# Four graph attention layers on one core: two groups of nodes are projected for layer 1 while layer 0 still gathers

## The chip, the cores and the metric

The kernel runs on one core of a Trainium2 chip. The metric is the device time of one execution in microseconds (us), from the first to the last instruction. Five engines work side by side, each through its own queue in order: TensorE (PE, matmuls; its weight loads are listed as PEld), VectorE (DVE), ScalarE (ACT), GpSimd (POOL) and SyncE (SP, which only starts transfers here). An engine that waits for a semaphore holds up all that stands behind in its queue.

## The reference

Four residual blocks over a graph of 3327 nodes with 256 features and a sparse symmetric adjacency with self loops (about 1% of the entries are set). Each is `x = layernorm(x + attention(x, adj))`:

```python
# layer 0: score_ij = sum_c a_c * leaky_relu(g_src[i,c] + g_tgt[j,c]);  softmax over j with adj_ij != 0;  weights @ g_tgt
x = layernorm(x + L0(x, adj))
# layer 1: Wh = x @ W.T; e_ij = leaky_relu(Wh_i.a1 + Wh_j.a2, 0.2); masked softmax; attention @ Wh
x = layernorm(x + L1(x, adj))
# layer 2: H = x @ W_fc + b; scores_ij = H_i.w1 + H_j.w2 (no leaky_relu); masked softmax; alpha @ H
x = layernorm(x + L2(x, adj))
# layer 3: two GAT layers with 4 heads of 64 features, each elu(masked softmax(leaky_relu(f1_i + f2_j)) @ h)
x = layernorm(x + L3(x, adj))
```

## The kernel before

Nodes are cut into 26 tiles of 128 (the last has 127). All arithmetic is float32 but for layer 2's sums, which take each feature as three bfloat16 parts.

**Layer 0 (`sparse0`)** doesn't form the dense scores, as they depend on all 256 channels of a pair. It finds each node's neighbours (`neighbours`, DVE), sorts the nodes of a group by their number of neighbours, and gathers the neighbours' rows from a table in DRAM: one indirect DMA on GpSimd for 128 rows (L527), 8 to a buffer `g` (L525), 11 buffers in turn. The nodes form three groups (`SETS`) of 5, 9 and 12 tiles. For each buffer DVE makes scores (L546, L552); at the end of a tile ACT takes the exponent and scales the gathered rows (L633), and PE sums them (L636, an identity as one operand). The result plus the input goes back to its place by an indirect DMA to `sums_d` (`put_back`, L671); once a group is whole it is read into `h` (`take`), and normalized (`finish_sums`, `finish_root`, `finish`). A hand-written table of due steps (`at_step`) sets the order: a step is one gather buffer. In this part the program's order is kept on PE, DVE, ACT and POOL.

**Layers 1 to 3 (`layers`)** are dense. With `leaky_relu` of a sum, exp(leaky(s_i + t_j)) splits: the weight of a pair is, up to a factor of the row that the softmax removes, `max(rate_i, q_j) * adj_ij`, times a factor that is put into the features of j. So DVE makes `e = max(rate, q) * at` in one instruction for a tile j and a block of rows (`weigh`, L1075), and PE adds `e.T @ feat` into PSUM (`one_head`, L1159; `many_heads`, L1198 and L1206 for the sums of the weights). The rows i form four blocks of 7, 7, 6 and 6 tiles; for each block the loop runs over all 26 tiles j. In layer 1 the adjacency comes as int32 (`at_i`, 448 KB a tile of 7), ACT turns it into bfloat16 and stores it (`at_d`, L1092), and the later layers read that.

A layer needs, of each tile of nodes, its features: `turn` transposes `h` on PE, ACT copies it (`ht`, L1107), `project` multiplies by the weights on PE (L1011) and ACT takes the exponents and scales (L1018, L1019, L1023). And it needs `rate`, a number for each node and head, laid out along the free axis and the same on every partition. `rates_of` makes it: a matmul with the source weights as the stationary operand gives rows of 1 or 4 partitions (L1048), ACT takes the exponent (L1053), SyncE writes the rows to DRAM (L1057) and reads them back as a broadcast to all partitions (L1064).

These preparations for the next layer are generators in a list `pending`; the main loops take one step of it after each tile j from the fifth on (`work_off`, `LATER`), or as many as are needed until a feature or a rate is there (`work_until`). For layer 1 there is no loop before it: the preparation of its first block stands alone between layer 0 and layer 1, and the other blocks' go between the first block's steps. In layers 1 and 2 PE alone is kept in the program's order, in layer 3 PE, DVE and ACT. In `finish_hidden`, which ends a block of the first of layer 3's two parts, the steps of a unit of two tiles are staged: `spread`, three steps later `scale` (which also sets off two ACT exponents), then `elu` on DVE (L1299) and `project`:

```python
yield from staged(units, [(0, spread), (3, scale), (4, elu), (5, project)])
```

After layer 3 a flag decides whether a dense fallback runs; with these inputs it doesn't.

Of the kernel before, what the change touches and what calls it, by code (L numbers as in the profile page):

```python
# [19 lines left out]
P = 128  # L20
# [26 lines left out]
def gat_stack(  # L47
# [55 lines left out]

    def copy_rows(engine, dst, src):

        rows = dst.shape[0]
        whole = rows // 16 * 16
        for lo, hi in ((0, whole), (whole, rows)):
            if lo < hi:
                engine.dma_start(dst[lo:hi], src[lo:hi])  # L110
# [7 lines left out]
    def load_row(work, src, name):  # L118

        size = src.shape[0]  # L120
        t = work.tile([P, size], F32, tag="row_" + name, name=name, bufs=1)
        nc.sync.dma_start(
            t, bass.AP(tensor=src.tensor, offset=src.offset, ap=[[0, P], [1, size]])
        )
        return t
# [124 lines left out]
    def sparse0(lost):  # L250
        GROUP, TURNS, LEAD = 8, 11, 4
        starts = [sum(SETS[:s]) for s in range(len(SETS))]
        with ExitStack() as s0:
# [21 lines left out]
            for c in range(kc):  # L275
                t = io0.tile([P, dim], F32, tag="hs", name="dots0")
                nc.vector.tensor_mul(t, w_tgt[:, c, :dim], a_row)
                nc.vector.tensor_reduce(w_tgt[:, c, dim : dim + 1], t, axis=AX.X, op=ALU.add)
# [228 lines left out]
            ]  # L507
            held = {}
# [4 lines left out]
            def gather(q):  # L513
                (s, t), k0, k1 = parts[q]
                if k0 == 0:
                    entry = held[s, t] = {"g": []}
                    lst = listed[s][:, t, :]
                    own = io0.tile([P, OWN], F32, tag="own", name="own_of", bufs=4)
                    nc.gpsimd.indirect_dma_start(
                        out=own[:, :], out_offset=None, in_=own_d[s][:, :],  # L520
                        in_offset=bass.IndirectOffsetOnAxis(ap=lst[:, KMAX : KMAX + 1], axis=0),
                    )
                    entry["lst"], entry["own"] = lst, own
                entry = held[s, t]
                g = gath.tile([P, GROUP, ROW], F32, tag=f"g{q % TURNS}", name="g")  # L525
                for k in range(k0, k1):
                    nc.gpsimd.indirect_dma_start(  # L527
                        out=g[:, k - k0, :], out_offset=None, in_=table_d[:, :],
                        in_offset=bass.IndirectOffsetOnAxis(
                            ap=entry["lst"][:, k : k + 1], axis=0  # L530
                        ),
                    )
                    if k % 2 and between:
                        between.pop(0)()
                entry["g"].append(g)
# [76 lines left out]
            def combine(s, t):  # L612
# [30 lines left out]
                for g, k0, m in groups[-1:] + groups[:-1]:  # L643
                    for k in range(m):
                        scale(g[:, k, :dim], k0 + k)
                    if m % 2:
                        singles.append(g[:, m - 1, :dim])
                    for k in reversed(range(0, m - 1, 2)):
                        left -= 1
                        add_up(acc, g[:, k : k + 2, :dim], left == kt // 2 - 1, left == 0)  # L650
                        while singles:
                            add_up(acc[:, len(singles) - 1, :], singles.pop(), False, False)
# [34 lines left out]
            def finish_sums(s):  # L687

# [4 lines left out]
                for k, it in enumerate(block):  # L693
# [3 lines left out]
                    nc.vector.bn_aggr(mv[:pn, k, :], stats[:pn])  # L697
                rstd = small.tile([P, max(SETS)], F32, tag="rstd0", name="rstd0", bufs=2)
# [10 lines left out]
            def finish(s):  # L709
                mv, rstd = moments.pop(s)  # L710
                for k in range(SETS[s]):
# [5 lines left out]
                    )  # L717

# [25 lines left out]
            for q, key in ends.items():  # L744
                at_step(q + 4, add_input, *key)
                at_step(q + 6, between.append, lambda key=key: put_back(*key))
                if key[1] == SETS[key[0]] - 1:
                    at_step(q + 10, take, key[0])
                    at_step(q + 13, finish_sums, key[0])
                    at_step(q + 16, finish_root, key[0])  # L750
                    at_step(q + 18, finish, key[0])
            for it in range(SETS[0]):
# [36 lines left out]
            assert not between  # L789

# [182 lines left out]
    def layers(rs):  # L973
# [16 lines left out]
        class Layer:  # L990


            def __init__(self, name, slot, nh, leaky, load, bias=None):
                self.slot, self.nh, self.leaky, self.bias = slot, nh, leaky, bias
                self.weight = work.tile([P, kc, dim + nh], F32, tag="weight", name=name + "w")
                row_src, row_dst = load(self.weight)
                dots(work, self.weight[:, :, dim : dim + nh], self.weight, row_dst, nh)
                if leaky:
                    self.w_src = work.tile([P, kc, nh], F32, tag="w_src", name="w_src")
                    dots(work, self.w_src, self.weight, row_src, nh)  # L1000
                    self.rate_d = dram.tile([heads, n], F32, name=f"rate_{slot}{nh}_d")
# [3 lines left out]
            def project(self, j, ht, banks):  # L1005
# [4 lines left out]
                for k in range(kc):  # L1010
                    nc.tensor.matmul(  # L1011
                        pacc[:pn, : dim + nh], ht[:, k, :pn], self.weight[:, k, :],
# [3 lines left out]
                if self.leaky:  # L1016
# [5 lines left out]
                    for lo in range(0, dim, width):  # L1022
# [3 lines left out]
                        )  # L1026
                else:
# [12 lines left out]
            def rates_of(self, b, ht, banks):  # L1040


                c0, c1 = cols_of(blocks[b])
                for lo in range(0, c1 - c0, BANK):
                    hi = min(lo + BANK, c1 - c0)
                    pr = misc(banks)
                    for k in range(kc):
                        nc.tensor.matmul(  # L1048
                            pr[: self.nh, : hi - lo], self.w_src[:, k, :], ht[:, k, lo:hi],
                            start=(k == 0), stop=(k == kc - 1),  # L1050
                        )
                    row = work.tile([heads, BANK], F32, tag="spread", name="rate_row", bufs=4)
                    nc.scalar.activation(  # L1053
                        row[: self.nh, : hi - lo], pr[: self.nh, : hi - lo], AF.Exp,
                        scale=1.0 - SLOPE,
                    )
                    nc.sync.dma_start(  # L1057
                        self.rate_d[: self.nh, c0 + lo : c0 + hi], row[: self.nh, : hi - lo]
                    )
# [3 lines left out]
                rows = self.rate_d[: self.nh, c0:c1]  # L1063
                nc.sync.dma_start(  # L1064
                    rate[:, : self.nh, : c1 - c0], rows[None].to_broadcast([P, self.nh, c1 - c0])
# [30 lines left out]
        def turn(b, banks):  # L1096

            ht = turn_p.tile([P, kc, wide], F32, tag="ht", name="ht")
            for it in blocks[b]:
                pn = rows_of(it)  # L1100
                at0 = (it - blocks[b][0]) * P
                tp = misc(banks)
                for k in range(kc):
                    nc.tensor.transpose(  # L1104
                        tp[:, k * P : k * P + pn], h[it][:pn, k * P : (k + 1) * P], ident[:pn, :pn]
                    )
                nc.scalar.copy(  # L1107
                    ht[:, :, at0 : at0 + pn],
                    tp[:, : kc * P].rearrange("p (k i) -> p k i", k=kc)[:, :, :pn],
                )  # L1110
                yield ht, it

        def prepare(nxt, b, banks, normed=True):
# [3 lines left out]
            for ht, it in turn(b, banks):  # L1117
                at0 = (it - blocks[b][0]) * P
                yield
                nxt.project(it, ht[:, :, at0 : at0 + P], banks)  # L1120
                yield
            if nxt.leaky:
                nxt.rates_of(b, ht, banks)
# [19 lines left out]
        def one_head(layer, nxt, banks_next):  # L1143

            for b, block in enumerate(blocks):
                work_until(lambda: not layer.leaky or layer.rate[b] is not None)
                accs = [bank(s) for s in range(len(block))]
                for j in range(nt):
# [17 lines left out]
                    if j >= LATER:  # L1166
                        work_off()
                work_until(lambda: not pending)
                for s, it in enumerate(block):
# [6 lines left out]
                    )  # L1176
                pending.append(prepare(nxt, b, banks_next, normed=False))
# [82 lines left out]
        def finish_hidden(b, o, sums):  # L1260
# [47 lines left out]
            yield from staged(units, [(0, spread), (3, scale), (4, elu), (5, project)])  # L1308
            l3b.rates_of(b, o, (6, 7))
# [61 lines left out]
        def load_plain(w, row_src, row_dst):  # L1371
            def load(t):
                nc.sync.dma_start(t[:, :, :dim], w.rearrange("(c p) f -> p c f", p=P))
                return load_row(work, row_src, "src"), load_row(work, row_dst, "dst")
# [3 lines left out]
        def load_heads(w, a):  # L1378
            def load(t):
# [6 lines left out]
                for s, name in enumerate(("src", "dst")):  # L1386
                    r = work.tile([P, dim], F32, tag="row_" + name, name=name, bufs=1)
# [12 lines left out]
        l1 = Layer("l1", "f", 1, True, load_plain(l1_w_t, l1_a[:dim], l1_a[dim:]))  # L1400
        for b in range(len(blocks)):
            pending.append(prepare(l1, b, (7,)))
        work_until(lambda: l1.rate[0] is not None and not pending)
        l2 = Layer(
            "l2", "g", 1, False, load_plain(l2_w, l2_att[:dim], l2_att[dim:]), load_row(work, l2_b, "bias")
        )
        rs.enter_context(tc.manual_schedule(engines={mybir.EngineType.PE}))
        one_head(l1, l2, (7,))
        l3a = Layer("l3a", "f", heads, True, load_heads(l3_w1, l3_a1))
        one_head(l2, l3a, (7,))  # L1410
# [7 lines left out]
        l3b = Layer("l3b", "g", heads, True, load_heads(l3_w2, l3_a2))  # L1418
# [6 lines left out]
    sparse0(lost)  # L1425
    with ExitStack() as rs:
        layers(rs)
# [75 lines left out]
```

The softmax here doesn't subtract the row's maximum and nothing guards it: scores larger than these inputs give would overflow.

## Time and profile before

Three runs gave 3260.0 to 3262.12 us, median 3261.68. The profiled execution has a span of 3261.5 us.

| engine | busy us | share of the span |
|---|---|---|
| PE | 2224.4 | 68% |
| PEld | 1218.1 | 37% |
| DVE | 2318.1 | 71% |
| ACT | 741.5 | 23% |
| POOL | 1029.6 | 32% |

The shares are means over stages that differ. By the slices of the page, layer 0 takes the first 1540 us, with PE at 10 to 50% and a TensorE clock of 0.5 to 0.7; from 1600 us on PE is busy at 90% or more at nearly full clock. The chain of work that ended last runs over PE for 46% of the span. A row of the costliest groups names line, engine, operation, output and inputs, the count, then busy time and the mean of one, then the engine's idle time just before and what ended it. DMA moves 364 MB in all, 112 GB/s on average.

### The profile page before, as it was taken

To read this page: it belongs to the slowest core of one execution; us is meant where nothing else is said; L and a number is where in the kernel's file an instruction comes from. 1 tells how busy PE (TensorE), PEld (TensorE's weight loads), DVE (VectorE), ACT (ScalarE), POOL (GpSimd) and SP (SyncE) were. 2 spreads that over 40 slices of the span, in tenths; PEclk is the share of its full clock that TensorE was granted. 3 is DMA by queue.
4 is the path that set the end of the run, shared out by engine and by line. 5 is a ranking of instruction groups with operands and counts; after the bars stand their busy time and mean duration, and the time that the engine had idled before them with its cause. 6 is when DMAs were issued, how large, how long until landed. Compare 5 with 4: busy or idle time off the path is not lost.

```text
span 3261.5 us, 44647 instructions
## 1 busy us (share of the span) xinstructions
PE 2224.4 (68%) x15644; PEld 1218.1 (37%) x15644; DVE 2318.1 (71%) x6589; ACT 741.5 (23%) x2002; POOL 1029.6 (32%) x1034
## 2 busy tenths in 40 slices
PE   3203332343441444343899999999999999999997
PEld 2101111121220221111478888774334444334342
DVE  6789999999975655554235642117888788899998
ACT  0003231342341343333334431110111110110110
POOL 0077657777767777774000000000000000000000
PEclk7556666666765776676699999999999999999998
DMA  7466536555435444443466753332212212212111
GB/s 216 137 141 180 169 100 150 173 157 155 112 86 109 124 111 113 113 113 91 125 199 199 201 161 93 100 99 72 63 44 68 61 46 65 63 49 57 56 47 48
DMA packets 176842, 364.21 MB, mean 112 GB/s; under 512 B 33746, under 2 KB 118964, under 8 KB 176610
## 3 DMA queue, kind: packets, MB, share of 16 engines
q1 hardware_dynamic: 96682, 183.56, 19.8%
q0 software_dynamic: 49632, 141.57, 16.9%
q10 hardware_dynamic: 30296, 36.15, 3.2%
q8 instruction: 126, 2.06, 0.3%
q14 instruction: 106, 0.87, 0.1%
HBM read 320.99 MB, written 43.58 MB: 112 GB/s over the span
## 4 chain that ended last, share of the span: by engine, by line
PE 46%; DVE 4%; DMA 2%; ACT 1%; issue 1%; DVEq 0%; SPq 0%; POOL 0%; ACTq 0%; POOLq 0%
PE acc L1198 17%; PE acc L1159 15%; PE acc L1206 8%; PE misc L1011 3%; DVE e L1075 3%; PE misc L1048 1%; DMA at_i<-in_adj_t_dram 1%; PE misc L1104 1%; DMA at<-at_d 1%; PE misc L1280 0%; PE misc L1241 0%; PE acc L636 0%; DVE stats L1355 0%; DVE h L1353 0%; ACT feat L1023 0%
## 5 line engine op out<-in xcount | busy, mean ns | idle before, releaser
L527 POOL DMA_INDIRECT g<-table_d,lst x923 | 912.6, 989 | 295.6 <-issue 268.8
L1075 DVE SCALAR_TENSOR_TENSOR e<-rate,feat,at 128x896 f32<-128x896 f32 (+4 forms) x832 | 843.1, 1078 | 67.7 <-PE acc L1206 58.4
L636 PE MATMUL acc<-g,ident 128*128 128x512 f32 (+1 forms) x934 | 454.7, 644 | 545.2 <-ACT g L633 512.7
L1198 PE MATMUL acc<-e,feat 128*32 128x384 f32 (+2 forms) x6656 | 722.8, 514 | 5.2 <-DVE e L1075 2.4
L225 POOL TENSOR_TENSOR rstds<-rstds,minus_half 128x7 f32<-128x7 f32 (+1 forms) x12 | 19.6, 1633 | 1671.7 <-DVE rstds L224 1671.7
L636 PEld LDWEIGHTS acc<-g,ident 128*128 128x128 f32 x934 | 193.3, 211 | 783.7 <-ACT g L633 561.6
L546 DVE TENSOR_TENSOR y<-g,both 128x1024 f32<-128x1024 f32 (+2 forms) x240 | 276.0, 1173 | 238.4 <-DMA g<-table_d,lst 223.5
L1206 PE MATMUL acc<-e,feat 128*32 128x384 f32 (+3 forms) x3328 | 397.5, 512 | 0.0
L1198 PEld LDWEIGHTS acc<-e,feat 128*32 128x32 f32 x6656 | 245.1, 109 | 381.8 <-issue 262.5
L633 ACT ACTIVATE g<-g,w 128x256 f32<-128x256 f32 x923 | 370.6, 494 | 0.0
L552 DVE SCALAR_TENSOR_TENSOR y<-y,both 128x256 f32<-128x256 f32 x923 | 324.5, 415 | 0.0
L1159 PE MATMUL acc<-feat,e 128*128 128x257 f32 (+2 forms) x1352 | 307.4, 381 | 0.6 <-DVE h L1173 0.6
L1159 PEld LDWEIGHTS acc<-feat,e 128*128 128x128 f32 (+2 forms) x1352 | 253.2, 190 | 39.7 <-issue 4.1
L1159 PE MATMUL acc<-feat,at 128*128 128x257 bf16 (+2 forms) x2028 | 240.9, 276 | 7.5 <-DMA at<-at_d 7.3
L466 PE MATMUL key_rows<-key_diag,ones 128*128 128x128 f32 x52 | 17.8, 440 | 314.5 <-DVE key_diag L465 259.5
L1159 PEld LDWEIGHTS <-at 128*128 128x128 bf16 (+2 forms) x2028 | 200.2, 100 | 43.9 <-DMA at<-at_d 8.0
L1075 DVE SCALAR_TENSOR_TENSOR e<-rate,feat,at_i 128x896 f32<-128x896 f32 (+2 forms) x104 | 112.2, 1081 | 143.1 <-DMA at_i<-in_adj_t_dram 109.8
L1206 PEld LDWEIGHTS acc<-e,feat 128*32 128x32 f32 (+1 forms) x3328 | 136.1, 110 | 164.2 <-issue 150.4
L421 DVE MAX8 cand<-num 128x8 f32<-128x64 uint16 x1352 | 178.9, 209 | 1.0
L542 ACT COPY both<-own_of 128x256 f32<-128x256 f32 x26 | 9.7, 374 | 602.1 <-DMA own_of<-own_d,lst 469.2
L466 PEld LDWEIGHTS key_rows<-key_diag,ones 128*128 128x128 f32 x52 | 12.1, 278 | 327.8 <-DVE key_diag L465 216.0
L1092 ACT CAST at<-at_i 128x896 bf16<-128x896 int32 (+2 forms) x104 | 92.0, 885 | 108.5 <-DMA at_i<-in_adj_t_dram 104.2
(158 smaller groups left out, 1707.5 us busy)
## 6 DMA issues: line engine op xcount, KB each, us to landing
at<-at_d SPq DMA_DIRECT2D x150, 224.0 KB
at_i<-in_adj_t_dram SPq DMA_DIRECT2D x50, 448.0 KB
adj_i<-in_adj_dram SPq DMA_DIRECT2D x25, 832.0 KB
adj_i<-in_adj_dram SPq DMA_DIRECT2D x25, 831.5 KB
g<-table_d,lst POOLq DMA_INDIRECT x923, 2.8
at<-at_d SPq DMA_DIRECT2D x75, 192.0 KB
at<-at_d SPq DMA_DIRECT2D x75, 191.8 KB
at_d<-at ACTq DMA_DIRECT2D x50, 224.0 KB
```

The lines of the kernel that those rows point to most:

```text
L421: nc.vector.max(cand[:, lo // CHUNK + c, :], v[:, c * CHUNK : (c + 1) * CHUNK])
L527: nc.gpsimd.indirect_dma_start(out=g[:, k - k0, :], out_offset=None, in_=table_d[:, :], in_offset=bass.IndirectOffsetOnAxis(ap=entry["lst" ...
L546: nc.vector.tensor_tensor(y, rows, minus_src[:, None, :].to_broadcast([P, m, dim]), op=ALU.max)
L552: nc.vector.scalar_tensor_tensor(y, y, 1.0, a, op0=ALU.mult, op1=ALU.mult, accum_out=sc)
L633: nc.scalar.activation(rows, rows, AF.Copy, scale=w[:, k : k + 1])
L636: nc.tensor.matmul(dst, ident, rows, start=start, stop=stop)
L1011: nc.tensor.matmul(pacc[:pn, : dim + nh], ht[:, k, :pn], self.weight[:, k, :], start=(k == 0), stop=(k == kc - 1),)
L1075: nc.vector.scalar_tensor_tensor(e[:pn, : c1 - c0], self.rate[b][:pn, h_of, : c1 - c0], q, at[:pn, : c1 - c0], op0=ALU.max, op1=ALU.mult,)
L1092: nc.scalar.copy(at[:pn, :w], at_i[:pn, :w])
L1159: nc.tensor.matmul(accs[s][:pn, : dim + 1], a[:pj, s * P : s * P + pn], f[:pj, : dim + 1], start=(j == 0 and part == 0), stop=(j == nt - 1 ...
L1198: nc.tensor.matmul(accs[x][p][q : q + 32, : hi - lo], f[:pj, at0 : at0 + 32], es[at0 // hd][:pj, lo:hi], start=(j == 0), stop=(j == nt - 1),)
L1206: nc.tensor.matmul(accs[x][pairs][h_of * 32 : (h_of + 1) * 32, : hi - lo], f[:pj, dim + h_of : dim + h_of + 1].to_broadcast([pj, 32]), es[ ...
```

## The change

Four things are changed together.

First, layer 1's projection of the first two groups (14 tiles, which are layer 1's blocks 0 and 1) moves into layer 0, between the gather steps of the third group. The weights are loaded and their two dot products made some steps ahead; then each tile has one step in which it is transposed and, two steps later, one in which it is projected. The features go to DRAM (`feats_d`), as the on-chip memory of layer 1 isn't free yet, and are fetched tile by tile, three ahead, in layer 1's first block. To give way, buffers `g` are numbered with a shift, and the last tile's sums run in ascending order.

Second, the last group's norms (`last_group`: read `h`, statistics, root, scaling) are no longer done before layer 1, but are steps of `pending` in the loop of layer 1's first block, which starts with the 14 tiles that are there; two steps are taken after each tile from the twelfth on. In this block DVE, ACT, POOL and SyncE too keep the program's order.

Third, rates are made otherwise: the source weights become further columns of the projection, ACT takes the exponent of that column per tile (`columns`), and at a block's end one matmul with the identity turns the columns into rows. The rows are written and read back through GpSimd's queue instead of SyncE's (in layer 0's part, written by SyncE).

Fourth, `elu` and `project` in `finish_hidden` come two steps later.

```diff
+            at = begins[len(SETS) - 1]
+            at_step(at - 6, load_next)
+            at_step(at - 3, dots_next, 0)
+            at_step(at - 2, dots_next, 1)
+            for s in range(len(SETS) - 1):
+                for it in range(starts[s], starts[s] + SETS[s]):
+                    at_step(at, turn_next, it)
+                    at_step(at + 2, project_next, it)
+                    at += 3
+                at = max(at, begins[len(SETS) - 1] + 19)
...
+            def last_group():
+                s = len(SETS) - 1
+                take(s)
+                for _ in range(4):
+                    yield
+                yield from settle(s)
+                finish_root(s)
+                yield
+                for lo in range(0, SETS[s], 6):
+                    finish(s, lo, lo + 6)
+                    yield
...
-            def rates_of(self, b, ht, banks):
...
+            def send_rates(self, b, banks):
+                m, t = misc(banks), self.nh * len(blocks[b])
+                nc.tensor.matmul(m[:t, :P], self.columns[:, :t], ident, start=True, stop=True)
+                row = work.tile([P, P], F32, tag="spread", name="rate_rows", bufs=4)
+                nc.scalar.copy(row[:t], m[:t, :P])
+                nc.gpsimd.dma_start(self.rate_d[b][:, :], row[:t])
+            def load_rates(self, b):
...
-                nc.sync.dma_start(
-                    rate[:, : self.nh, : c1 - c0], rows[None].to_broadcast([P, self.nh, c1 - c0])
+                nc.gpsimd.dma_start(
+                    rate[:, : self.nh, :],
+                    rows[None].to_broadcast([P, self.nh, len(blocks[b]) * P]),
...
             if nxt.leaky:
-                nxt.rates_of(b, ht, banks)
+                nxt.send_rates(b, banks)
+                yield
+                yield
+                nxt.load_rates(b)
...
-                    if j >= LATER:
+                    if layer is l1 and b == 0:
+                        work_off(2 if j > 10 else 1)
+                        fetch([j + 3])
+                        if j > early and late:
+                            l1.load_rates(late.pop(0))
+                    elif j >= LATER:
                         work_off()
...
-            yield from staged(units, [(0, spread), (3, scale), (4, elu), (5, project)])
-            l3b.rates_of(b, o, (6, 7))
+            yield from staged(units, [(0, spread), (3, scale), (6, elu), (7, project)])
+            l3b.send_rates(b, (6, 7))
+            yield
+            yield
+            l3b.load_rates(b)
...
-        l1 = Layer("l1", "f", 1, True, load_plain(l1_w_t, l1_a[:dim], l1_a[dim:]))
-        for b in range(len(blocks)):
-            pending.append(prepare(l1, b, (7,)))
-        work_until(lambda: l1.rate[0] is not None and not pending)
...
+        if early:
+            l1.load_rates(late.pop(0))
+        fetch(range(3))
+        if rest is not None:
+            pending.insert(0, rest)
```

`turn_next` and `project_next` do for one tile what `turn` and `project` do in `layers`, and store the 258 columns of features; `settle` is `finish_sums` with a pause after each three tiles; `early` is 14 and `rest` is `last_group()`.

## The prediction

> **What bounds the kernel now.** I read the table of stretches first, then the chain that ended last over the seam between layer 0 and layer 1, then the chain over one block of layer 2, then DVE's timeline in a layer 3 block.
>
> Stretches (us, busy us and count of each engine, granted TensorE clock, DMA share, GB/s):
>
> ```profile
> 960.00:1516.00 556.00, 211.76 (x448) 95.31 (x448) 309.49 (x1160) 186.37 (x477) 421.39 (x444) 0.68 0.44 114
> 1516.00:1541.00 25.00, 14.85 (x28) 6.17 (x28) 7.80 (x36) 11.28 (x29) 1.99 (x2) 0.69 0.10 20
> 1541.00:1599.00 58.00, 34.23 (x69) 15.71 (x70) 17.21 (x52) 11.97 (x42) 3.27 (x2) 0.53 0.34 103
> 1599.00:1706.00 107.00, 105.16 (x473) 82.02 (x472) 33.99 (x38) 46.19 (x102) 0.00 (x0) 1.00 0.65 191
> 1706.00:1940.00 234.00, 233.42 (x1097) 203.33 (x1096) 130.08 (x258) 93.62 (x174) 4.27 (x3) 1.00 0.69 198
> 1940.00:2222.00 282.00, 272.45 (x2219) 227.43 (x2218) 45.66 (x166) 43.38 (x176) 5.60 (x4) 0.99 0.35 98
> 2222.00:2745.00 523.00, 518.68 (x5339) 215.84 (x5338) 443.28 (x475) 62.81 (x223) 2.09 (x1) 1.00 0.21 57
> ```
>
> Row 1 is the third group of layer 0: POOL is busy 421 of 556 us, one gather of 0.95 us every 1.25 us, so GpSimd's issue sets the pace while PE and ACT are over half idle. Row 3 is the seam: 58 us at a clock of 0.53 in which nothing of layer 1's sums runs. From row 4 on PE is busy 97 to 100%: layers 1 to 3a are bound by PE, and what is taken from PE there is taken from the time.
>
> The chain through the seam (start, us, what):
>
> ```profile
> 1528.51 11.94 PE acc L636 x24
> ...
> 1541.03 0.44 DVE hs L664
> 1541.75 2.74 DMA sums_d<-hs,lst
> 1544.74 2.85 DMA l1w<-in_l_w_t_dram
> 1547.60 3.64 DMA l2w<-in_l_w_dram
> ...
> 1577.15 2.09 PE misc L1011 x4
> 1579.50 0.45 ACT feat L1023
> 1580.00 3.59 PE misc L1048 x4
> 1583.67 0.59 ACT rate_row L1053
> 1584.31 2.73 PE misc L1048 x4
> ...
> 1598.83 0.85 PE acc L1159 x2
> ```
>
> PE ends layer 0 at 1540.4; layer 1's first sum starts at 1598.8, after the weights, ten projections of about 4.0 us each at the low clock, and the rates.
>
> A block end in layer 2:
>
> ```profile
> 2075.04 1.82 PE misc L1048 x4
> ...
> 2076.88 0.59 ACT rate_row L1053
> ...
> 2077.52 1.45 PE misc L1048 x4
> 2078.98 4.82 PE acc L1159 x43
> 2083.80 6.30 DMA at<-at_d
> ```
>
> The rate rows take 3.9 us of PE's time, and then PE waits for an adjacency tile whose load stands behind the rate's load on SyncE's queue (1792 KB, issued at 2081.89; `at` follows at 2083.80 and lands 6.30 us later). DVE in layer 3a:
>
> ```profile
> 2423.48 0.69 DVE L1299 SCALAR_TENSOR_TENSOR o<-spreads,o 128x512 f32<-128x512 f32 x1 [5.46 <-ACT spreads L1258]
> ```
>
> DVE stands 5.46 us for ACT's exponent before it can make the next e tiles.
>
> **What the Trainium skill says.** "TensorE: Matmul & The Clock Gate", Part 1 (What's actually happening): the array runs at half clock until a window of some 3.4 us is busy. The trace agrees: four projection matmuls cost 2.09 us in the seam and 0.87 after 1600. "DMA: Bandwidth & Descriptors", Issuing engines are not separate DMA queues: loads from any engine share the same 16 DMA engines. So GpSimd's queue adds no bandwidth, only another order; no row of before shows rate loads there. The same page, Anatomy of one DMA: about 2.0 us fixed plus bytes/436e3; gathers of before land after 2.8 us (median), `lst` (348 KB) after 4.5.
>
> **The change part by part.**
>
> *Early projection (14 tiles).* Transposes, projections, feature copies and small exponents of 14 tiles move into row 1. ACT does 0.37+3x0.17+0.47 = 1.35 us a tile, 19 us; PE at the low clock 0.70+2.09, 39 us. ACT has 370 us idle there, PE 344. What is queued behind them is the next tile's scaling and sums, which come 4 or more gather groups (about 40 us) apart; so the gathers don't see it. DVE's dots (8 x 0.4 = 3.2 us) fall where DVE is at 56 to 81%. Layer 0: +1 us, between 0 and +8 if DVE or ACT hold a gather buffer.
>
> *The seam.* In the changed order the first loads of layer 1 on SyncE still wait for DVE's last sum (1541.5), and the first rate load stands on GpSimd behind the last put-back. Put-back 1541.75 + 0.97, issue of the rate load 0.93 (the `lst` row), then 448 KB: 2.0 + 459/436 = 3.05 us by the skill's price (estimate), while SyncE's load of the same rate before took 4.4 us from issue (1588.72) to its e (1593.11). I take 4.4: landed at 1548.3, e 1.15 us, first sum 1549.5 instead of 1598.8.
>
> *The first block of layer 1.* Before, from 1598.8 to 1706.1 (DVE's first L1172), 107 us: 26 steps x 14 matmuls x 0.2174 = 79 us, 19 projections (0.22+0.87), rates 9.1 (busy time of L1048 there). After: 79 + 12 x (0.25+0.5+0.9) where 0.5 is the wait for ACT between transpose and projection (0.46 in the seam; half of the 12 have sums between), so 17, + 0.5 for two turned rates = 97 us if PE is fed. It is not quite: for the first 14 steps a step needs 448 KB in, 224 KB out and 129 KB of saved features, 0.82 MB, and besides h (1.57 MB), two rates (0.9) and early weights (0.65): 14.6 MB. At 250 GB/s (the upper slices of this stretch run 240 to 280) that is 58 us against 43 us of PE. The h loads also stand on ACT between the casts of tiles 0 and 1, and SyncE's third and fourth tile wait behind those (about 5 us). I add 3 us of cold clock and 10 of hunger: 110 us, end at 1659.5 instead of 1706.1. **-46 us** (ends: PE fed -57, transfers at 200 GB/s and a slow GpSimd load -28). The norms of the last group (12 x 0.6 + 12 x 0.33 us on DVE, 2.3 us on POOL) lie beside PE's first 11 steps, as e leaves DVE 1.9 us a step.
>
> *Rates turned by block.* Layer 2's stretch has 24 L1048 matmuls, 9.6 us of PE, plus three ACT gaps of 0.68: 11.6; new are three turns of about 0.25. **-10.9**. In 2222 to 2850 L1048 has 12.0 + 2.7 us; new five turns. **-13.4**. The extra exponent (0.17 us a tile on ACT) and the 4 extra columns (some 0.02 us a matmul) lie beside or cost under 1 us.
>
> *Rates on GpSimd's queue.* The three waits for `at` in layer 2 (PE waits 7.3 us by the list of waits) come from one queue's order. POOL does only 6 us there, so nothing stands behind its own waits but a norm's root. **-7.3**, 0 if sharing the DMA engines costs the same.
>
> *elu two steps later.* DVE waits 42.6 us in 10 pieces for L1258. On PE: step from 2426.11 to the next projection 6.1 us instead of 4.51; from 2438.74 6.8+ after two; in block 1 gaps of 1.9, 2.7, 2.0. About 5.6 and 6.6 us a block, 22 over four. With the wait gone DVE needs 4.3+0.7 us a step, below PE's 6. The last steps come later but 20 fit into 23. I take **-17** (ends -22, -5). Layer 3b is bound by DVE in part and stays.
>
> Sum: +1 -46 -10.9 -13.4 -7.3 -17 = -93.6; 3261.7 - 93.6 = 3168.
>
> **Rivals.**
> A: transfers bound the new first block. The rate and feature loads, h, weights and 8 outstanding transfers collide; the seam gives 28, the queue change 0, elu 10: -28+1-10.9-13.4-10 = -61, 3200. For it: 191 GB/s at a share of 0.65 already; against: slices at 250 and more.
> B: PE is fed at once, elu gives all: -57-10.9-13.4-7.3-22 = -111, 3151. For it: PE reached 100% when it had e tiles; against: the feed count above.
> C: slower. The early work stands in PE's and ACT's fixed order; if each of 28 turns and projections held back the gathers by the 4.0 us that such a tile took in the seam plus a gather, 28 x 5 = 140, against 94 gained: 3308. Against it: of POOL's idle time before a gather in row 1, nearly all is its own issue (0.30 us each).
>
> **How the numbers follow.** Main case 0.56, A 0.22, B 0.16, C 0.04, no change 0.02. The time is the main case's, 3168. The range leaves out C and the ends of A and B: 3140 to 3204. Faster 0.94, same 0.02, slower 0.04.
>
> **What would show it.** Right: the first sum of layer 1 some 9 us after layer 0's last; its block ending 105 to 115 us on; no wait of PE for `at` in layer 2; no DVE wait for ACT before elu; the gathers' pace still 1.25 us. Wrong: PE waiting for e in steps 3 to 13 by more than 15 us in sum; gathers waiting for ACT or PE in the third group; the last gather later than 1520; PE in layer 3a now waiting for DVE.

## The result, and the profile after

The changed kernel takes 3184.9 us (median of 4 runs, 3182.11 to 3187.85) against 3261.9 for the kernel before in the same session: a ratio of 0.9764, with a 95% interval from 0.9747 to 0.9781, or 77 us gained. The profiled executions have spans of 3181.0 and 3261.5 us, 80.5 us apart; the accounts by stretch below are of these two.

The stretches of the changed kernel (us, then busy us and count of PE, PEld, DVE, ACT and POOL, granted TensorE clock, DMA share, GB/s):

```profile
960.00:1515.00 555.00, 238.40 (x536) 110.71 (x536) 315.57 (x1184) 200.55 (x549) 420.45 (x444) 0.69 0.46 118
1515.00:1541.00 26.00, 14.20 (x28) 6.33 (x28) 8.28 (x36) 11.28 (x29) 2.95 (x4) 0.71 0.11 21
1541.00:1554.00 13.00, 0.05 (x1) 0.08 (x1) 1.15 (x1) 0.94 (x1) 1.41 (x2) 0.61 0.65 204
1554.00:1662.00 108.00, 96.88 (x429) 79.32 (x430) 38.40 (x64) 35.58 (x87) 4.33 (x5) 0.98 0.67 203
1662.00:1755.00 93.00, 87.75 (x408) 75.38 (x407) 53.34 (x104) 37.49 (x65) 2.37 (x3) 1.00 0.70 211
1755.00:1906.00 151.00, 150.41 (x707) 131.29 (x706) 83.67 (x171) 59.65 (x114) 2.80 (x2) 1.00 0.67 196
1906.00:2173.00 267.00, 259.26 (x2200) 222.75 (x2198) 46.97 (x171) 42.30 (x193) 9.02 (x10) 1.00 0.37 105
2173.00:2668.00 495.00, 492.40 (x5311) 232.87 (x5315) 442.98 (x473) 62.30 (x247) 6.41 (x9) 0.99 0.22 61
```

Row 1 is the third group of layer 0. PE has 88 matmuls more there, and POOL has the same 444 gathers in the same time. Row 3 is what is left of the seam: 13 us where there were 58. In row 5 PE is idle for 5 of 93 us, in a block that had none idle before.

Each block ends with DVE's first reciprocal of the sums (layers 1 and 2) or with ACT's first copy of the weights' sums (layer 3). The time of each block between these marks, read from the timelines:

| us | before | after | change |
|---|---|---|---|
| start to the end of layer 0's last sum (DVE) | 1541.5 | 1540.6 | -0.9 |
| from there to the first sum of layer 1 | 57.1 | 13.4 | -43.7 |
| layer 1, block 0, from its first sum | 107.5 | 108.2 | +0.7 |
| layer 1, blocks 1, 2, 3 | 87.4, 74.9, 75.0 | 93.1, 75.7, 75.0 | +5.7, +0.8, 0 |
| layer 2, blocks 0 to 3 | 67.7, 73.0, 68.1, 70.2 | 67.7, 69.5, 62.5, 67.1 | 0, -3.5, -5.6, -3.1 |
| layer 3a, blocks 0 to 3 | 140.6, 139.5, 124.0, 120.1 | 136.2, 131.6, 115.1, 112.7 | -4.4, -7.9, -8.9, -7.4 |
| layer 3b, blocks 0 to 3 | 136.1, 129.3, 113.6, 111.5 | 129.4, 129.3, 113.6, 111.6 | -6.7, 0, 0, 0 |
| from the last mark to the end | 24.4 | 28.8 | +4.4 |

The chain through the seam (start, us, what):

```profile
1540.84 2.42 DMA sums_d<-hs,lst
...
1545.14 6.83 DMA at_i<-in_adj_t_dram
...
1552.05 0.95 ACT at L1212
```

The weights and the ten projections are gone from it; the landing of the last put-back and one adjacency tile remain, and PE starts at 1553.95.

The end of layer 2's second block, by the chain of waits:

```profile
2037.62 0.33 PE misc L1172 x2
2037.95 7.15 PE acc L1279 x63
...
2045.12 5.57 DMA at<-at_d
```

The old rate matmuls (3.9 us) have become one turn of 0.33 us. The wait for an adjacency tile behind it is still there. PE's sums of layer 2 on the two pages, before and after, with the idle time of PE before them at the end of the row:

```profile
L1159 PE MATMUL acc<-feat,at 128*128 128x257 bf16 (+2 forms) x2028 | 240.9, 276 | 7.5 <-DMA at<-at_d 7.3
L1279 PE MATMUL acc<-feat,at 128*128 128x257 bf16 (+2 forms) x2028 | 236.4, 273 | 7.0 <-DMA at<-at_d 6.7
```

DVE's elu, from the groups by line of layer 3, before and after (busy us, mean ns, idle time before):

```profile
L1299 DVE SCALAR_TENSOR_TENSOR o<-spreads,o 128x512 f32<-128x512 f32 (+2 forms) x14 | 9.1, 651 | 42.6 <-ACT spreads L1258 42.6
L1427 DVE SCALAR_TENSOR_TENSOR o<-spreads,o 128x512 f32<-128x512 f32 (+2 forms) x14 | 9.1, 647 | 0.0
```

Its waits for ACT, ten pieces before, are gone.

### The profile page after: what moved, and what is told of

Its sections match the earlier page's. It is cut to its first block, busy times and chain, and to the rows that moved or that the text cites. A ratio compares the mean times of both kernels' runs of the same rounds, so it can differ in the third digit from the quotient of the medians.

```text
span 3181.0 us, 44618 instructions
## 1 busy us (share of the span) xinstructions
PE 2170.4 (68%) x15572; PEld 1239.5 (39%) x15572; DVE 2316.7 (73%) x6592; ACT 734.7 (23%) x2068; POOL 1042.3 (33%) x1056
## 3 DMA queue, kind: packets, MB, share of 16 engines
q8 instruction: 125, 2.05, 0.3%
## 4 chain that ended last, share of the span: by engine, by line
PE 45%; DVE 4%; DMA 1%; issue 0%; ACT 0%; POOL 0%; ACTq 0%; SPq 0%; DVEq 0%; POOLq 0%
PE acc L1326 17%; PE acc L1279 15%; PE acc L1334 8%; DVE e L1195 3%; PE misc L1125 3%; DMA at_i<-in_adj_t_dram 1%; DMA at<-at_d 1%; PE misc L1222 0%; PE misc L1408 0%; PE misc L1369 0%; DVE h L246 0%; DVE stats L1486 0%; DVE h L1484 0%; DVE h L1299 0%; DVE both L1481 0%
## 5 line engine op out<-in xcount | busy, mean ns | idle before, releaser
L1326 PE MATMUL acc<-e,feat 128*32 128x384 f32 (+2 forms) x6656 | 689.0, 516 | 4.8 <-DVE e L1195 2.1
L1326 PEld LDWEIGHTS acc<-e,feat 128*32 128x32 f32 x6656 | 259.2, 110 | 343.2 <-issue 233.8
L1334 PE MATMUL acc<-e,feat 128*32 128x384 f32 (+3 forms) x3328 | 375.6, 513 | 0.0
L1279 PEld LDWEIGHTS acc<-feat,e 128*128 128x128 f32 (+2 forms) x1352 | 255.4, 191 | 63.7 <-issue 15.4
L1334 PEld LDWEIGHTS acc<-e,feat 128*32 128x32 f32 (+1 forms) x3328 | 139.3, 110 | 155.3 <-issue 131.8
L1195 DVE SCALAR_TENSOR_TENSOR e<-rate,feat,at_i 128x896 f32<-128x896 f32 (+2 forms) x104 | 111.1, 1079 | 94.9 <-ACT feat L1133 54.6
L481 PEld LDWEIGHTS key_rows<-key_diag,ones 128*128 128x128 f32 x52 | 12.2, 278 | 324.9 <-DVE key_diag L480 214.3
```

Of the source, the lines that this page charges most:

```text
L481: nc.tensor.matmul(key_rows[:, t * P : (t + 1) * P], ones, key_diag, start=True, stop=True)
L1195: nc.vector.scalar_tensor_tensor(e[:pn, : c1 - c0], self.rate[b][:pn, h_of, : c1 - c0], q, at[:pn, : c1 - c0], op0=ALU.max, op1=ALU.mult,)
L1279: nc.tensor.matmul(accs[s][:pn, : dim + 1], a[:pj, s * P : s * P + pn], f[:pj, : dim + 1], start=(j == 0 and part == 0), stop=(j == nt - 1 ...
L1326: nc.tensor.matmul(accs[x][p][q : q + 32, : hi - lo], f[:pj, at0 : at0 + 32], es[at0 // hd][:pj, lo:hi], start=(j == 0), stop=(j == nt - 1),)
L1334: nc.tensor.matmul(accs[x][pairs][h_of * 32 : (h_of + 1) * 32, : hi - lo], f[:pj, dim + h_of : dim + h_of + 1].to_broadcast([pj, 32]), es[ ...
```

## The experiments

Times are medians; where a kernel is an edit of the changed one, it is held against 3184.9 us (ratio 0.9764 to the kernel before). Blocks and waits are those of each run's profiled execution. From run to run a block comes out the same within 1.5 us where neither it nor the one before it was changed; only layer 2's third and fourth, in which waits for `at` fall, move by some 3 us.

**elu alone, in the kernel before.**

```diff
-            yield from staged(units, [(0, spread), (3, scale), (4, elu), (5, project)])
+            yield from staged(units, [(0, spread), (3, scale), (6, elu), (7, project)])
```

> The kernel before with one edit: elu and project two steps later. Theory (the wait of DVE for ACT's exponent really held PE): the four blocks that carry it (three of layer 3a, the first of 3b) lose about 18 us together, 3262 to 3244 (14 to 22 gained), and DVE no longer waits for ACT ahead of its elu step. Rival (DVE has to do this work anyway and PE was covered): 5 us gained or less, 3257 or more, and the gain of those blocks in the changed kernel is from the rates.

It took 3239.4 us, ratio 0.9935 (0.9920 to 0.9951), 21 us gained. The four blocks became 134.3, 117.8, 115.0 and 131.7 us, 5.2 + 6.2 + 5.1 + 4.4 = 20.9 us less; all other blocks of layer 3 stayed within 0.2 us. DVE no longer waits ahead of this step. So about half of its 42.6 us of waits had held PE as well.

**Layer 3b's rates the old way, in the changed kernel.** `finish_hidden` calls a `rates_of` like the old one, on the columns of the source weights; its transfers go through GpSimd.

```diff
-            l3b.send_rates(b, (6, 7))
-            yield
-            yield
-            l3b.load_rates(b)
+            l3b.rates_of(b, o, (6, 7))
```

> The changed kernel with only layer 3b's rates made the old way (matmuls of the turned block against the source columns, four exponents' rows), elu still late. Theory (PE pays for these matmuls in full): the four blocks that carry them get some 3.3 us longer each, 13 us in sum (10 to 15), 3198. Rival (they fall into PE's waits for DVE): 4 us or less, 3189.

It took 3196.3 us, ratio 0.9805 (0.9790 to 0.9820), 11 us slower than the changed kernel. The four blocks took 134.4, 117.8, 115.1 and 131.8 us: 2.8 + 2.7 + 2.4 + 2.4 = 10.3 us more than in the changed kernel, and the same to 0.1 us as in the kernel before with the late elu. So the two parts add without touching each other: 20.9 + 10.3 = 31.2, against the 30.9 that these four blocks lost.

**The early work done twice.**

```diff
                     at_step(at, turn_next, it)
+                    at_step(at + 1, turn_next, it)
...
                 project(p, ht, P, w1)
+                project(p, ht, P, w1)
```

> The changed kernel with every early transpose, its copy, and every early projection done twice. Theory (the third group of layer 0 hides them): the last sum of layer 0 stays at 1540 us within 1.5 us and the whole within 2 us, 3183 to 3187. Rival (they hold gathers back, which the first time was hidden by luck): about 28 pieces of 0.4 to 2 us appear in part, 10 to 40 us slower, 3195 to 3225.

It took 3184.5 us, ratio 0.9769 (0.9755 to 0.9782), and layer 1's first sum came at 1552.3 us. Twice the transposes, copies and projections cost nothing that can be measured; the early work is hidden with room to spare.

**The rates back on SyncE.**

```diff
-                nc.gpsimd.dma_start(self.rate_d[b][:, :], row[:t])
+                nc.sync.dma_start(self.rate_d[b][:, :], row[:t])
...
-                nc.gpsimd.dma_start(
+                nc.sync.dma_start(
                     rate[:, : self.nh, :],
```

> The changed kernel with the stores and loads of the rates back on SyncE's queue. Theory (the wait for the adjacency tile in layer 2 comes from the 1792 KB rate load filling the DMA engines, whichever queue issues it): within 2 us of the changed kernel, 3183 to 3187, three waits of PE for it of about 2.3 us each as now. Rival (the prediction's: order on one queue makes the wait): 7 us slower than the changed kernel, 3192.

It took 3189.9 us, ratio 0.9782 (0.9769 to 0.9796): some 5 us slower, with intervals that overlap. The place is clear from the blocks of the profiled execution, which is 8.6 us longer. Layer 2's were 67.7, 69.5, 63.2 and 67.8 us, 1.4 us more than in the changed kernel, with PE's waits for `at` 8.4 us in sum against 6.7. Layer 1's first block took 122.9 us from its first sum instead of 108.2. SyncE's timeline in it (start, us, engine, line, transfer):

```profile
1600.70 0.33 SPq L122 DMA_DIRECT2D at_i<-in_adj_t_dram  x1
1622.21 0.28 SPq L1175 DMA_DIRECT2D rate_d<-rate_rows  x1
1622.61 0.33 SPq L122 DMA_DIRECT2D at_i<-in_adj_t_dram  x1
```

SyncE stands for 21 us at the store of a block's rates, which PE turns only at 1621.45, and the adjacency loads stand behind it. PE then waits 5.4 us for the next e tile:

```profile
1627.23 3.37 PE L1279 MATMUL acc<-feat,e 128*128 128x257 f32 x7 [5.40 <-DVE e L1195]
```

So the queue change is worth something, but in layer 1, where transfers are held in written order, and not in layer 2. Neither of the two expectations had that. The block's 14.7 us are more than the whole shows, as some came back elsewhere: 4.7 us after the last mark (24.1 us to the end instead of 28.8) and some 3.5 before layer 1's first sum and in its second block.

**Only one head's rate loaded.** The other three heads' rates are set to 1, which leaves out part of layers 3a and 3b.

```diff
+                if self.nh > 1:
+                    nc.gpsimd.memset(rate[:, 1 : self.nh, :], 1.0)
                 nc.gpsimd.dma_start(
-                    rate[:, : self.nh, :],
-                    rows[None].to_broadcast([P, self.nh, len(blocks[b]) * P]),
+                    rate[:, :1, :],
+                    rows[None, :1].to_broadcast([P, 1, len(blocks[b]) * P]),
                 )
```

> The changed kernel with only the first head's rate loaded in layers 3a and 3b (448 KB or less a block instead of 1792); the other three heads' rates are set to 1 by GpSimd, which leaves out part of the computation. In the run with four transfers GpSimd issued all four within 2.2 us, so that run didn't spread the bytes; this one takes them away. Theory (the bytes of the rate load hold up the adjacency tile in layer 2): PE's waits for it fall from 6.7 us to 2 or less, layer 2's second to fourth block from 199 us to 194. Rival (the tile would be late there for another cause, such as the work at a block's end): the waits stay at 5 us or more.

Layer 0 took 404 us longer in this run, and the kernel before, at 3661.6 us in the same session, was slower by as much; so only the stretch from layer 1 on is compared. Layer 2's blocks took 67.8, 69.5, 60.7 and 61.3 us: 191.5 for the second to fourth, against 199.1. The row of PE's sums in layer 2:

```profile
L1281 PE MATMUL acc<-feat,at 128*128 128x257 bf16 (+2 forms) x2028 | 236.1, 273 | 0.6 <-DMA at<-at_d 0.4 <-DVE h L1301 0.2
```

The wait for `at` is 0.4 us where the changed kernel has 6.7. The load still leaves at the same place, 4.7 us after PE's turn of the rates (5.4 in the changed kernel). So the bytes of the rate load make the wait.

**The rate load cut in four.**

```diff
-                nc.gpsimd.dma_start(
-                    rate[:, : self.nh, :],
-                    rows[None].to_broadcast([P, self.nh, len(blocks[b]) * P]),
-                )
...
+                for x in range(self.nh):
+                    nc.gpsimd.dma_start(
+                        rate[:, x : x + 1, :],
+                        rows[None, x : x + 1].to_broadcast([P, 1, len(blocks[b]) * P]),
+                    )
...
+                    yield
```

> The changed kernel with each rate load of four heads (1792 or 1536 KB in one transfer) given out as four transfers of one head, one a step. Theory (that one transfer fills the DMA engines for 7 us, and the adjacency tile of layer 2 that is due then waits with it): the three waits of PE in layer 2 (6.7 us in sum) fall to 2 or less, 5 us gained, 3180. Rival (the total of bytes decides, or the tile waits for something else): waits as before, within 1.5 us.

It took 3180.0 us, ratio 0.9760 (0.9746 to 0.9773), which the interval doesn't tell from the changed kernel; the waits for `at` were 7.3 us in four pieces. The theory's 3180 was met by luck: what became shorter in the profile is the stretch from the last mark to the end, 24.2 us instead of 28.8, and layer 2's last block became 2.6 us longer. GpSimd's timeline shows why it settles nothing on spacing:

```profile
2040.26 2.15 POOL L1184 DMA_DIRECT2D rate<-rate3a_d  x4 [2.87 <-DMA rate3a_d<-rate_rows]
```

All four were issued within 2.15 us, as the program has nothing on GpSimd that waits for PE's steps there. Loads truly spread over the steps weren't tried.

The stretch at the end is GpSimd's. It closes the program with a DRAIN, listed here with its least, median and longest time in ns and the starts of the first and last of three; the longest is the first. The changed kernel, then the cut load:

```profile
L1627 POOLq DRAIN  x3: 50/103/9546, 3170.5 to 3180.6; - x3
L1628 POOLq DRAIN  x3: 50/103/2522, 3170.2 to 3177.4; - x3
```

In the changed kernel it ends at 3180.0, 27.8 us after the last mark; SyncE is through its last stores at 23.7, and the other engines wait for GpSimd. In all runs with the rates on GpSimd and the loads whole it ends 27.8 to 28.2 us after the mark. With the rates on SyncE, and in the kernel before, it takes 7.75 us and ends at 23.1, and with the cut loads at 19.1; the end is then SyncE's.

**Layer 3a's rows in a buffer of their own.** In the second block of layer 1, SyncE's timeline of the changed kernel shows:

```profile
1658.72 0.38 SPq L1519 DMA_DIRECT2D src<-in_l_a_dram  x1
1667.73 0.38 SPq L1519 DMA_DIRECT2D dst<-in_l_a_dram  x1
1668.21 2.15 SPq L122 DMA_DIRECT2D at_i<-in_adj_t_dram  x4
```

The row `dst` of layer 3a takes the place of a row of layer 2, which DVE uses for its dot products only after the block's end (L151, at 1666.95); for 9 us the adjacency loads stand behind it.

```diff
+                if own:
+                    both = turn_p.tile([P, heads // 2, wide], F32, tag="ht", name="rows3")
...
+                    if own:
+                        r = both[:, s, :dim]
+                    else:
...
-        l3a = Layer("l3a", "f", heads, True, load_heads(l3_w1, l3_a1), rate_d=rate3_d[0])
+        l3a = Layer("l3a", "f", heads, True, load_heads(l3_w1, l3_a1, True), rate_d=rate3_d[0])
```

> The changed kernel with layer 3a's two attention rows in a buffer of their own, free at that time, instead of the shared four. Theory (in the second block of layer 1 the adjacency loads stood on SyncE behind the load of such a row, which waited for its buffer until DVE had used the old one): the row and the adjacency loads behind it leave about 9 us earlier, PE's idle time from 1662 to 1683 falls from 5 us to 1 or less, 5 us gained (4 to 7), 3180. Rival (transfers bound the start of this block, 225 GB/s there): PE's idle time stays, within 1.5 us of the changed kernel.

It took 3183.1 us, ratio 0.9759 (0.9746 to 0.9773), not told apart by the interval. The block took 90.8 us instead of 93.1, and PE's idle time at its start fell from 5.2 us (0.31 + 1.18 + 2.05 + 1.66) to 2.9. In the other runs that leave the first block as it is, this block took 92.4 to 93.1 us. So the row explains some 2 of the 5.7 us that it had lost; the rest stayed, and the result lies between the two expectations.

**Work one piece ahead in the first block.** The chain of the changed kernel in the last six steps of that block reads, for each:

```profile
1630.61 0.89 PE misc L1125 x4
...
1631.52 0.17 ACT feat L1132
1631.69 0.07 ACT feat L1133
...
1631.78 1.16 DVE e L1195
...
1632.99 3.30 PE acc L1279 x14
```

The projection of tile j comes just before the sums that need e(j), so PE, ACT, DVE and PE work in series: 5.68 us a step.

```diff
-                        work_off(2 if j > 10 else 1)
+                        work_off(2 if j > 9 else 1)
```

> The changed kernel with two pieces of the waiting work a step from step 10 of the first block on instead of step 11, so that each projection is one piece further ahead of the sums. Theory (in the last six steps the chain projection, ACT, DVE's e, sums runs in series, 5.68 us a step, since the features are made just in time; in the six before, ACT's copy of the turned tile holds PE for 0.46 us): these twelve steps become 4.15 and 4.86 us, 9 us gained (6 to 11), 3176. Rival (the adjacency loads can't come faster): 2 us or less.

It took 3180.6 us, ratio 0.9753 (0.9740 to 0.9767): 4 us less by the medians, and block 0 105.2 us instead of 108.2. The last six steps fell to 4.86 us, as expected; but the six before rose from 4.86 to 5.18, since now a projection came directly before the next turn, and that waits until ACT has read their common PSUM bank (L1150, the last to read it). Neither the theory nor the rival had this.

**The last group's sums loaded over four steps.**

```diff
-                take(s)
-                for _ in range(4):
+                for lo in range(0, SETS[s], 3):
+                    take(s, lo, lo + 3)
                     yield
```

> The changed kernel with the last group's twelve sums loaded three at a time over four steps instead of all between the casts of steps 0 and 1. Theory (they hold ACT's second cast and, by the buffers, SyncE's fourth adjacency load): the time from the first sum of layer 1 to PE's unbroken run falls from 13.2 us by about 4, 3181. Rival (the first 26 us move 235 GB/s and the next 27 us 332; the transfers themselves bound this stretch): within 1 us of the changed kernel.

It took 3184.8 us, ratio 0.9765 (0.9751 to 0.9778): the rival's number. PE's busy time from 1541.0 to 1594.5 us was 38.71 us against 38.68. PE had 1.2 us more by 1567 and 1.2 us less from there on. What these waits are bound by stays open; the rival's transfers fit, but no run took bytes away here.

**The last three together.** The diff is the three above.

> The last three edits together. Theory (three separate waits): the gains add, 5 + 9 + 4 = 18 us, 3167. Rival (they share the DMA engines as their common limit): the best of the three alone at most, some 3176.

It took 3180.2 us, ratio 0.9751 (0.9738 to 0.9765). Block 0 took 105.9 us and block 1 87.8, 7.6 us less than in the changed kernel. In layer 2 the waits for `at` were 9.9 us instead of 6.7; over the changed kernel and all its edits whose rate load is whole they lie between 6.7 and 9.9 us, so that some 3 us come and go for a cause that stays open. The gains didn't add, but the rival's ground, a common limit of the transfers, isn't shown by this.

**Work in the middle of a step.** With a turn (the transposing of a tile) and a projection side by side, either order pays ACT. So one goes between the step's sums:

```diff
                     for s, it in enumerate(block):
+                        if s == 4 and layer is l1 and b == 0 and j > 9:
+                            work_off()
...
-                        work_off(2 if j > 10 else 1)
+                        work_off()
```

> The changed kernel with the waiting work of the first block given out one piece after the fourth of a step's seven sums and one at its end, from step 10 on, instead of two at its end from step 11. Theory (two pieces side by side pay ACT each time, as they share one PSUM bank: 0.46 us between a turn and its projection, 1.2 us between a projection and the next turn): with sums between them both waits are hidden and the features are a step ahead; a step is 3.03 + 0.22 + 0.89 = 4.15 us against 4.86 and 5.68, so 10 to 13 us gained by the end of the first block, 3173. Rival (adjacency loads can't keep 4.15 us a step, or a later stall takes it back as in the last edit of this kind): 4 us, 3181.

It took 3169.5 us, ratio 0.9720 (0.9707 to 0.9734), 15 us less than the changed kernel. Its chain:

```profile
1590.40 0.22 PE misc L1222 x2
1590.62 1.74 PE acc L1281 x8
1592.36 0.87 PE misc L1125 x4
1593.23 1.30 PE acc L1281 x6
```

A step is 4.13 us and all of it is PE's; block 0 took 93.4 us instead of 108.2. Two things are in this edit: it also begins one step earlier, which alone gave 3.0 us of the 14.8 in the run one piece ahead. And the expectation lays both waits to the PSUM bank, but a projection also needs ACT's copy of the turned tile, so only the wait in the other order speaks for the bank.

**Mid-step work, own rows and the cut load together.** The diff is the three above.

> Mid-step work, split rate loads, and layer 3a's rows in a buffer of their own, together. Theory (separate waits in separate stretches): 11 + 5 + 2 = 18 us gained, 3167. Rival (what is gained in the first block is lost at the start of the second, where adjacency loads are late): 8 us or less, 3177.

It took 3165.0 us, ratio 0.9709 (0.9695 to 0.9722), 20 us below the changed kernel and 96 below the one before. Block 0 took 94.9 us, block 1 89.5, and the waits for `at` were 5.6 us. It is the fastest version here. Its profiled execution is 6.4 us below that of mid-step work alone: 3.5 of them are again after the last mark (25.3 us instead of 28.8), and 3.2 are waits for `at`, which vary by as much from run to run. So what the cut load is seen to give lies at the end, and not in layer 2 as expected.

## Why the prediction was right, and where it was not

The direction and the range held, and most parts came where they were expected; the forecast of -93.6 us was 13 us too good for the profiled execution (-80.5). Of the signs that were named, the first sum some 9 us after layer 0's last (it was 13.4) and the end of PE's waits for `at` (6.7 us are left) did not come; a first block of 105 to 115 us, no wait of DVE before elu, and gathers 1.25 us apart did.

*Early projection, +1.* Layer 0 ended 0.9 us earlier, and doing the transposes, copies and projections twice changed nothing. Right, and shown.

*Seam and first block, -46.* Measured -44.0 at the end of the block (1662.1 against 1706.1), from parts that were partly wrong. The first sum came at 1553.95 instead of 1549.5: the first loads waited for the put-back to land (2.42 us), where I had them leave without it, and the first adjacency tile took 6.83 us to land, on which I had set no time of its own, since I took the rate's load (4.4 us) for the last to arrive. From there the block took 108 us where I had 110, and this agreement is luck. My 110 us were PE's bare work, 3 us of waits for ACT, 3 for the cold clock and 10 for hunger (PE waiting for adjacency tiles). PE's first runs:

```profile
1553.95 8.00 PE L1279 MATMUL acc<-feat,e 128*128 128x257 f32 x28 [14.43 <-DMA at_i<-in_adj_t_dram]
1562.89 3.30 PE L1279 MATMUL acc<-feat,e 128*128 128x257 f32 x14 [0.94 <-DVE e L1195]
1567.12 27.57 PE L1279 MATMUL acc<-feat,e 128*128 128x257 f32 x126 [0.93 <-DVE e L1195]
```

The 42 matmuls of the first 13.2 us are worth 9.1 at 0.2174 each, so cold clock and hunger took 4.0 together, where I had 13. Against them, six steps took 4.86 us and six 5.68 where PE's own work is 4.13 (the mid-step run): 13.7 us lost to the waits for ACT between turn and projection and to the serial chain of the last six steps, where I had 3. A run of matmuls after such a wait also takes longer itself (a projection's four 1.14 us instead of 0.89, a step's fourteen 3.30 instead of 3.03). The mid-step run took back 14.8 us with the same transfers to make. So the largest loss there was the placing of the work, which I had nearly left out, and I had laid the loss to hunger.

*Not in the sum: block 1, +5.7, and block 2, +0.8.* I followed the new loads on SyncE through the first block and not past its end. A row that waited for its buffer held the adjacency loads: some 2 us, by the run with a buffer of its own. The rest stays open; with mid-step work the block still took 89.8, and 87.8 only with own rows, work one piece ahead and the sums loaded over four steps together.

*Rates turned by block, -10.9 and -13.4.* Layer 2 fell by 12.2 us, of which 0.6 is the difference in waits for `at`, so -11.6. Its second block, in which no such wait falls, is the cleaner measure: 3.5 us less, and the same in every edit of the changed kernel, where the estimate has 3.6 a block. No run changes layer 2's part alone. In layer 3: 10.3 us in the run with the old rates of 3b; the 4.4 that 3a's first block lost, in which the rates of 3a's last block are made, are put down to them without a run of their own: 14.7. Both right in the mechanism and near in size.

*Rates on GpSimd's queue, -7.3.* This step failed. I had laid the wait for `at` to the order on one queue. The waits are 6.7 us instead of 7.3, still there with the load on another queue, and gone (0.4 us) when three quarters of its bytes are. The Trainium skill, in "DMA: Bandwidth & Descriptors" under Issuing engines are not separate DMA queues, says just this, that transfers run on the same 16 DMA engines whoever starts them. I had quoted it and kept 0 only as an end of the range, where it was the value to take. The change of queue helps in one place and costs in another. In layer 1's first block, where the store of the rates would hold the adjacency loads, it is worth 14.7 us, a benefit that was inside my estimate of the block, unnamed; at the end it costs 4.7. By the medians of the whole some 5 us are left.

*elu two steps later, -17.* Measured -20.9 alone, near my end of -22. The mechanism was right and the estimate low.

*The end, not in the sum.* From the last mark to the end it took 28.8 us instead of 24.4. The instructions up to the stores come at the same distances; then GpSimd's closing DRAIN takes 9.55 us instead of 7.75, begins 2.9 us later (18.3 us after the mark instead of 15.4), and ends last. It is a price of the rates on GpSimd's queue: with that one edit taken back the tail is 24.1 us. The bytes don't set it, as it is 9.55 us with one head's rate too. Why it takes longer with these loads, and less when they are cut in four, stays open.

The differences to the forecast, in us: layer 0, seam and first block +1.0, blocks 1 and 2 +6.5, layer 2 +6.0, layer 3 -4.9 (35.3 gained against 30.4), the end +4.4: 13.0 together.

By the number alone rival A (3200) lies as near to 3184.9 as the main case (3168). It was right in one thing: the queue gives layer 2 nothing. Its other terms were not: the seam and the first block gave 44 us where it had 28, elu 20.9 where it had 10, and its main claim, that transfers bound the first block, fits the first 13 us at most.

## What to carry to other kernels

Where an engine's order is written by hand, place each producer by its whole chain (PE, ACT, DVE, PE) and not only by its count per step: two pieces of side work next to each other pay the other engine's time, and with main work between them they pay nothing. Ask of each transfer put into a queue what it waits for itself, for its buffer or for its data, and what stands behind it; a load that waits for bandwidth isn't helped by another queue. And follow a change one block past the one that it is meant for.

## What the runs showed of the hardware

While one transfer of 1536 or 1792 KB by GpSimd was under way (7.3 to 8.0 us from issue to landing), an adjacency tile of 192 KB, which lands in a median of 2.4 us, took 5.4 to 5.8 us. With the same bytes in four transfers issued within 2.15 us it took 5.0 to 6.8 us.

A projection directly after a turn began 0.46 us late, ACT's copy of 0.38 us, which it reads, lying between. A turn directly after a projection, in the same PSUM bank, began 0.83 us late in the last six steps of the changed kernel.

GpSimd's closing DRAIN took 7.75 us with no rate load on its queue, 9.55 to 9.87 with whole loads and 2.52 with loads cut in four.
